# Normalising and turning the second batch's tokens during the first batch's value projection, and choosing PSUM banks by an expected clock

## The chip, the cores and the metric

One core of a Trainium2 chip runs the whole kernel. The metric is the device time of one execution in microseconds (us). Five engines work side by side, each through its own list of instructions in the order in which the program writes them: TensorE (PE) multiplies and transposes into PSUM, VectorE (DVE), ScalarE (ACT) and GpSimd (POOL) work elementwise, and SyncE (SP) only issues DMAs. GpSimd issues DMAs too. An instruction waits until what it reads is written and what it overwrites is read; whatever stands behind it on its engine waits with it.

## The reference: what is computed

`x` has the shape (2, 1024, 1024): two batches of 1024 tokens. All is float32.

```python
xn  = layernorm(x)                                  # no weights
qkv = clip(xn @ Wqkv.T, -8, 8); q, k, v = split(qkv, 3)
q = layer_norm(q, q_ln_w, q_ln_b); k = layer_norm(k, k_ln_w, k_ln_b)
# 32 heads of 32 channels
scores = q @ k.T * 32**-0.5 + slopes * (key - query)    # ALiBi, causal
attn = softmax(scores) @ v
ffn  = xn @ (mean(abs(W), axis=1) * sign(W)).T + bias
out  = x + attn @ Wout.T + ffn
```

## The kernel before, in words

**Projections.** q, k, v and the output projection take seven products instead of eight for each pair of 128-token tiles. The first operand is a pair tile, [128 channels, 7 factors, 4 blocks of channels, 128 tokens]: the tokens, turned so that channels lie on the partitions, as four quarters (A11, A12, A21, A22) and four sums of them (S1 to S4; S3 takes A21's place). `seven` (L413) issues 4 matmuls for each of the seven factors in the order 11, 21, t2, t3, t4, t1, 22 (L210); `combine` (L434) puts the results together on VectorE and ScalarE, with the clip. The weights of a projection, 28 tiles of [128, 512], come through a ring of 28 buffers; `load_weights` (L332) puts the next load on SP's queue when a tile of the projection before has been used for the last time. So k of batch 1 gets its weights while the last pair of v of batch 0 is computed.

**x.** `normalize_x` (L541) takes statistics of a tile on VectorE (L497, L503), the reciprocal root on ScalarE (L507) with a Newton step on VectorE (L513 to L516), and scales on ScalarE (L520). `turn_x` (L546) turns the tile with eight PE transposes (L527, in `transposed`, L524) into two PSUM banks, copied by ScalarE into the pair tile (L554). GpSimd forms the four sums (`add_up`, L399 to L409) and stores the pair tile to DRAM, `xd` (L559, L561, L568), in the layout of the pair tile. q and v, and much later the binarised layer (`prepare`, L755), load it back (`load_pair`, L577). For batch 0 this happens during its k projection, at the start of the kernel. For batch 1 two tiles are loaded and normalised near the end of batch 0's v (in `values`, L663); the rest, all turns, sums and stores lie inside batch 1's k projection.

**k and q.** After the projection, `to_channels` (L584) normalises a row tile, turns it on VectorE in two instructions that transpose every 32x32 block of 128x512 (L592), and stores it with four GpSimd DMAs of 128 KB (L598), whose place in DRAM completes the turn.

**Order of the program.** It is written out by hand. `pieces` (L917) is one long generator: k, q and v of batch 0, the same of batch 1, the binarised layer, the output projection. `fill(time)` (L927) draws from it, counted in the planner's expected times (0.915 us for a projection matmul). The list `sides` holds smaller generators (a tile's normalising, turning, storing); `advance_sides` (L351) moves each by one step for every two pieces. Before the loop over the attention steps the program fills k, q and all but the last 70 matmuls of v of batch 0 (L1270). Then each step issues the loads of keys three steps ahead (`load_keys`, L955), the scaling of keys on ScalarE (`scale_keys`, L964), the first scores (`first_scores`, L1037: four PSUM banks written by PE at L1046, row maxima by VectorE at L1062), the shifts of a block when its maxima are done (`shifts`, L1074: arithmetic on GpSimd, a small PE transpose `trs` at L1088, rows on VectorE), and for the block 9 steps back the second scores (`second_scores`, L1098: PE L1108 and L1122, mask on VectorE L1141, exp on ScalarE L1150), the weighing of values (`weigh_values`, L1181, PE L1190) and the division (`divide`, L1204). Between these, `fill` adds projection matmuls, in a share per step that spreads the projections of batch 1 over the steps (L1256).

**PSUM.** One bank holds the weighed values; the other seven are one rotating pool, and `score_bank` (L372) takes the next in turn for scores, projections (`fill_tile`, L375), transposes (L524) and `trs` (L1088).

Of the kernel before, what the change touches and what calls it, by code (L numbers as in the profile page):

```python
# [19 lines left out]
EPS = 1e-5  # L20
MASKED = -3.0e38
LOWEST = -3.4e38


@with_exitstack
def parallel_block_kernel(
# [33 lines left out]

    nc = tc.nc
    B, S, D = x.shape
    P = 128
    NT = S // P
# [15 lines left out]
    slopes = [2.0 ** (-(h + 1) * ALIBI_BIAS_MAX / N_HEADS) for h in range(N_HEADS)]  # L82

    ctx.enter_context(tc.manual_schedule())
    const = ctx.enter_context(tc.tile_pool(name="const", bufs=1))
    pair_pool = ctx.enter_context(tc.tile_pool(name="pair", bufs=2))
    wpool = ctx.enter_context(tc.tile_pool(name="w", bufs=RING))
    group = ctx.enter_context(tc.tile_pool(name="group", bufs=3))
    work = ctx.enter_context(tc.tile_pool(name="work", bufs=2))
    small = ctx.enter_context(tc.tile_pool(name="small", bufs=4))  # L90
    dram = ctx.enter_context(tc.tile_pool(name="dram", bufs=2, space=bass.MemoryType.DRAM))
    ps_s = ctx.enter_context(tc.tile_pool(name="ps_s", bufs=7, space=bass.MemoryType.PSUM))
    ps_o = ctx.enter_context(tc.tile_pool(name="ps_o", bufs=1, space=bass.MemoryType.PSUM))


    nc.scalar.preload_act_table_set("natural_log_exp_and_others")


    ident = const.tile([P, P], FP, tag="ident", name="ident")
    make_identity(nc, ident)  # L100
    ident_b = const.tile([P, P], BF, tag="ident_b", name="ident_b")
    nc.vector.tensor_copy(ident_b, ident)
    minus_b = const.tile([P, P], BF, tag="minus_b", name="minus_b")
# [111 lines left out]
    def half(n):  # L215
        return slice(n * HALF, (n + 1) * HALF)
# [115 lines left out]
    def load_weights(count):  # L332

        room[0] += count
        while todo and todo[0][0] <= room[0]:
            cost, do = todo.pop(0)
            room[0] -= cost
            do()
# [30 lines left out]
    def half_tile(name):  # L369
        return work.tile([P, HALF], FP, tag="half", name=name, bufs=2)  # L370

    def score_bank(name):  # L372
        return ps_s.tile([P, HALF], FP, tag="s", name=name)

    def fill_tile(name):  # L375
        return score_bank(name)
# [1 line left out]
    def tokens(t):  # L378
        return slice(t * P, (t + 1) * P)

    kd, qd, vd, od, xd = ({} for _ in range(5))
    for b in range(B):
        for what, d in (("k", kd), ("q", qd), ("o", od)):
            d[b] = dram.tile([NC, P, S], FP, tag=f"{what}d", name=f"{what}d_{b}")
        for p in range(NT // 2):
            xd[b, p] = dram.tile([P, 8, NI, P], FP, tag=f"xd{p}", name=f"xd_{b}_{p}")
        vd[b] = dram.tile([S, D], FP, tag="vd", name=f"vd_{b}")

    A11, A12, A22, S3, S1, S2, S4 = range(7)
    A21 = S3
    FACTOR = {"11": A11, "21": A12, "t2": S2, "t3": S3, "t4": A22, "t1": S1, "22": S4}

# [126 lines left out]
            )  # L522

    def transposed(src, c0, what):  # L524
        ps = ps_s.tile([P, 4, P], FP, tag="s", name=f"tr_{what}_{c0}")
        for j in range(4):
            nc.tensor.transpose(  # L527
                ps[:, j, :], src[:, (c0 + j) * P : (c0 + j + 1) * P], ident
            )
        return ps  # L530
# [4 lines left out]
    def load_x(b, t):  # L535
        xin[b, t] = io_tile(f"x_{b}_{t}")
        nc.sync.dma_start(xin[b, t], x[b, tokens(t), :])
# [8 lines left out]
    def turn_x(b, t):  # L546
        p = t // 2
        if t % 2 == 0:
            pairs[b, p] = pair_tile(f"xT_{b}_{p}")
        pr, d = pairs[b, p], xd[b, p]  # L550
        src = xn.pop((b, t))
        for c0, k in ((0, (A11, A21)[t % 2]), (NI, (A12, A22)[t % 2])):
            ps = transposed(src, c0, f"x{b}_{t}")
            nc.scalar.copy(pr[:, k, :, :], ps)  # L554
            yield Turn(TURN) if c0 == 0 else TURN
        if t + 2 < NT:
            load_x(b, t + 2)
        if t % 2 == 0:
            nc.gpsimd.dma_start(d[:, 1:3], pr[:, A11 : A12 + 1])  # L559
        else:  # L560
            nc.gpsimd.dma_start(d[:, 0], pr[:, A21])  # L561
            if (b, p) == (0, 0):
                add_up(pr, nc.vector, 0, NI, lambda: load_weights(NI))
            else:
                add_up(pr, nc.vector if b == 0 and p == 1 else nc.gpsimd, 0, NI)
            done.add(("x", b, p))
            yield 0.0
            nc.gpsimd.dma_start(d[:, 3:], pr[:, A22:])  # L568

    def layernorm(b, t):  # L570
        yield from normalize_x(b, t)
# [9 lines left out]
    W32 = 32  # L581
    BLOCKS = D // W32

    def to_channels(what, b, t, raw, d):  # L584

        name = f"{what}{b}_{t}"
        yield from spread(raw, stats_of(raw, name), name)
        yield 0.0
        dst = work.tile([P, BLOCKS, W32], FP, tag="io", name=f"{what}T_{b}_{t}", bufs=5)
        for n in range(NH2):  # L590
            at = slice(n * BLOCKS // NH2, (n + 1) * BLOCKS // NH2)
            nc.vector.transpose(dst[:, at, :], raw[:, half(n)])  # L592
            yield 0.0
        rows = d[b][:, :, tokens(t)].rearrange("c p s -> (c p) s")
        rows = rows.rearrange("(k r) s -> r k s", r=W32)
        for a in range(P // W32):
            at = slice(a * W32, (a + 1) * W32)
            nc.gpsimd.dma_start(rows[:, :, at], dst[at, :, :])  # L598
        if t == NT - 2:
            done.add((what, b))  # L600

    def projected(what, b, ready):

        if what == "k":
            if b == 0:
                load_x(b, 0)
                load_weights(NI)
                load_x(b, 1)
                load_weights(3 * NI)
                yield from normalize_x(b, 0)  # L610
            yield from turn_x(b, 0)
            if b == 0:
                yield from normalize_x(b, 1)
                load_weights(NI)
        for p in range(NT // 2):
            more = p + 1 < NT // 2
            if what == "k" and more:
                if p > 0:
                    sides.append(layernorm(b, 2 * p + 2))
            elif what != "k" and more:  # L620
                load_pair(b, p + 1)
            elif what in "kq":
                load_pair(b, 0)
            elif b + 1 == B:
                early.extend((signs(), prepare(*every_tile[0])))
                sides.extend(early)
            if (what, b, p) == ("k", 0, 1):
                sides.append(ahead())
            name = f"{what}{b}_{p}"
            rows = [raw_tile(f"{what}raw_{b}_{2 * p + i}") for i in range(2)]  # L630

            def whole(i, src, p=p):
                ready(2 * p + i, src)

            take = combine(name, *rows, whole, bound=CLIP_QKV)
            pr = pairs[b, p]
            args = pr, name, f"{what}{b}", not more, take
            yield from seven(*args, ORDER[:1])
            if what == "k" and p == 0:
                yield from turn_x(b, 1)  # L640
                third = layernorm(b, 2)
                if b == 0:
                    load_weights(1)
                    next(third)
                    load_weights(NI - 1)
                sides.append(third)
            yield from seven(*args, ORDER[1:2])
            if what == "k" and more:
                sides.append(layernorm(b, 2 * p + 3))
            assert ("x", b, p) in done  # L650
            yield from seven(*args, ORDER[2:])
# [11 lines left out]
    def values(b):  # L663
        if b > 0:
            sides.append(residual())

        def ready(t, rows):
            nc.gpsimd.dma_start(vd[b][tokens(t), :], rows)
            if t == NT - 3 and b + 1 < B:
                for i in range(2):  # L670
                    load_x(b + 1, i)
                    sides.append(normalize_x(b + 1, i))
            if t == NT - 2:
                done.add(("v", b))

        return projected("v", b, ready)
# [78 lines left out]
    def prepare(b, t):  # L755

        xt = work.tile([P, NC, P], FP, tag="io", name=f"xt_{b}_{t}", bufs=5)
        d = xd[b, t // 2]
        if t % 2 == 0:
            nc.sync.dma_start(xt.rearrange("p (k c) q -> p k c q", k=2), d[:, 1:3])  # L760
        else:
            nc.sync.dma_start(xt[:, :NI], d[:, 0])
            nc.sync.dma_start(xt[:, NI:], d[:, 3])
        yield 0.0
        hl = []
        for c0 in range(0, NC, NI):
# [307 lines left out]
    def shifts(b, qb, g):  # L1074
# [9 lines left out]
        nc.gpsimd.tensor_tensor(low, sh, mid, ALU.subtract)  # L1084
        yield True

        ps = ps_s.tile([P, P], BF, tag="s", name=f"trs_{b}_{qb}_{g}")
        nc.tensor.transpose(ps, shift_b, ident_b)  # L1088
        rows = small.tile([P, HALF], BF, tag="rows", name=f"rows_{b}_{qb}_{g}", bufs=4)
        nc.vector.tensor_tensor(  # L1090
# [162 lines left out]
    proj = NT // 2 * len(ORDER) * NI * ONE  # L1253


    fills = 3 * proj + AHEAD * ONE + 2 * NT * TURN  # L1256
    share = (fills + sum(time_of(n) for n in range(middle))) / middle
    fills = 1.5 * proj + 2 * ONE + B * NT * 8 * SHORT - BEHIND * ONE
    each = fills / (steps - middle)
# [7 lines left out]
    for n in range(3):  # L1267
        if n in opens:
            load_keys(*opens[n])
    fill(proj - AHEAD * ONE)  # L1270
    chains = []
    for n in range(2):
        if n in opens:
            scale_keys(*opens[n])
    for n in range(steps + 1):
        if n + 3 in opens and not short_lead(opens[n + 3]):
            fill_until(("q", opens[n + 3][0]))
# [88 lines left out]
```

## Time and profile before

| what | us |
|---|---|
| runs, three | 1538.0, 1540.42, 1540.76 |
| their median | 1540.42 |
| the profiled execution's own time | 1538.28 |
| its span, from the first to the last instruction | 1536.5 |
| VectorE turns of keys, 128x512, median | 0.70 |
| landing of the first weights' form, `w_k`, median | 5.6 |
| landing of `xp<-xd`, 1792 KB, median | 8.1 |

The profile is of one execution. A line of it names an engine, the line of the kernel (L527), the operation, and the tiles as output<-input; `idle <- releaser` is how long the engine stood still before it and whose end let it go on. A matmul in float32 leaves two records in the trace. PE's clock was granted at 0.996 on the mean. The DMA lines give, for each kind of transfer, its queue (SPq, POOLq), count, size and the median time to landing:

```profile
xp<-xd SPq DMA_DIRECT2D x16, 1792.0 KB, 8.1
kg<-kd SPq DMA_DIRECT2D x48, 256.0 KB, 4.9
vg<-vd SPq DMA_DIRECT2D x48, 256.0 KB, 5.6
...
xd<-xT POOLq DMA_DIRECT2D x8, 1280.0 KB, 5.2
x<-in_x_dram SPq DMA_DIRECT2D x16, 512.0 KB, 6.1
kd<-kT POOLq DMA_DIRECT2D x64, 128.0 KB, 4.3
```

### The profile page before, as it was taken

How to read it: one execution, taken by the hardware profiler on the slowest of the kernel's cores; microseconds unless marked ns; L12 is line 12 of the kernel's file. 1: busy time of each engine (PE TensorE's matmuls, PEld its weight loads, DVE VectorE, ACT ScalarE, POOL GpSimd, SP SyncE). 2: the span in 40 equal slices, each digit the busy share in tenths (PEclk: the TensorE clock that was granted, in tenths of full speed). 3: DMA queues.
4: the chain of work that ended last, by engine and by line, in shares of the span. 5: the costliest groups of instructions: out<-in, count | busy, mean ns of one | idle time of the engine just before them, and what ended most of it. 6: DMA issues, size and time to landing. Idle time of an engine off the chain costs nothing.

```text
span 1536.5 us, 24276 instructions
## 1 busy us (share of the span) xinstructions
PE 1495.2 (97%) x8100; PEld 636.6 (41%) x8100; DVE 965.9 (63%) x2714; ACT 637.9 (42%) x1219; POOL 1019.2 (66%) x1308
## 2 busy tenths in 40 slices
PE   7999999999999999999999999999999999999998
PEld 3444444444334333333333334555555333333333
DVE  6856553778687766766765565766655565565332
ACT  3322110115556445344444375555555344444430
POOL 4587283025677675796775599877788887777661
PEclk9999999999999999999999999999999999999999
DMA  7788364582333844569842286666668233312232
GB/s 294 273 286 289 95 231 145 194 313 93 114 97 127 260 151 162 102 153 288 260 151 94 106 255 217 144 143 164 144 164 217 72 90 97 88 39 67 59 80 55
DMA packets 118958, 244.88 MB, mean 159 GB/s; under 512 B 12081, under 2 KB 52529, under 8 KB 115505
## 3 DMA queue, kind: packets, MB, share of 16 engines
q1 hardware_dynamic: 90912, 148.94, 28.9%
q0 software_dynamic: 27920, 94.39, 24.9%
q8 instruction: 64, 1.05, 0.3%
q14 instruction: 62, 0.50, 0.1%
HBM read 155.47 MB, written 107.74 MB: 171 GB/s over the span
## 4 chain that ended last, share of the span: by engine, by line
PE 81%; DVE 9%; ACT 4%; issue 3%; POOL 2%; DMA 1%; POOLq 0%; DVEq 0%; ACTq 0%
PE s L1046 9%; PE mm_f L817 8%; PE s L1122 8%; PE mm_q_t L419 8%; PE o L1190 7%; PE mm_o_t L419 7%; PE mm_k_t L419 6%; PE mm_o L419 5%; PE mm_v_t L419 5%; PE mm_v L419 4%; PE mm_q L419 4%; PE mm_k L419 3%; PE s L1108 3%; DVE s L1062 3%; PE den L1209 2%
## 5 line engine op out<-in xcount | busy, mean ns | idle before, releaser
L1179 POOL TENSOR_TENSOR pT<-pT,pT 128x512 f32<-128x512 f32 (+3 forms) x628 | 577.9, 977 | 161.8 <-ACT pT L1150 140.7
L1150 ACT ACTIVATE pT<-s,kpos 128x512 f32<-128x512 f32 (+3 forms) x768 | 378.2, 590 | 440.0 <-DVE s L1141 255.7
L1062 DVE CUSTOM_DVE_ANT_0 s<-s,rel 128x512 f32<-128x512 f32 (+3 forms) x512 | 283.3, 600 | 90.4 <-PE s L1046 84.7
L1046 PE MATMUL s<-kg,qg 32*128 32x512 f32 (+3 forms) x1536 | 174.4, 520 | 0.0
L1062 DVE CUSTOM_DVE_ANT_0 s<-s,rel,mx 128x512 f32<-128x512 f32 (+3 forms) x256 | 140.8, 589 | 42.4 <-PE s L1046 40.1
L1122 PE MATMUL s<-qg,kg 32*128 32x512 f32 (+3 forms) x1536 | 159.6, 495 | 0.0
L1190 PE MATMUL o<-pT,vg 128*32 128x512 f32 (+3 forms) x1536 | 156.3, 494 | 1.3 <-ACT pT L1150 1.3
L817 PE MATMUL mm_f<-sg,hl 128*128 128x512 f32 x512 | 126.7, 399 | 1.7 <-DVE mx L1062 1.7
L1141 DVE TENSOR_TENSOR s<-s,behind 128x256 f32<-128x256 f32 (+1 forms) x320 | 97.9, 374 | 36.9 <-PE s L1122 36.8
L419 PE MATMUL mm_o_t<-w_o_t,ot 128*128 128x512 f32 x256 | 116.5, 602 | 0.0
L1046 PEld LDWEIGHTS s<-kg,qg 32*128 32x128 f32 x1536 | 71.0, 183 | 104.3 <-issue 56.4
L419 PE MATMUL mm_k_t<-w_k_t,xT 128*128 128x512 f32 x224 | 108.9, 614 | 0.0
L419 PE MATMUL mm_v_t<-w_v_t,xp 128*128 128x512 f32 x224 | 106.3, 607 | 2.7 <-POOL w_v_t L236 2.7
L1062 DVE DVE_READ_ACCUMULATOR2_ANT mx<- 128x1 f32 x768 | 108.7, 141 | 0.0
L419 PE MATMUL mm_q_t<-w_q_t,xp 128*128 128x512 f32 x224 | 107.7, 618 | 0.0
L817 PEld LDWEIGHTS mm_f<-sg,hl 128*128 128x128 f32 x512 | 93.4, 188 | 33.6 <-DVE mx L1062 12.0
L1108 PE MATMUL s<-rows,minus_b 12*128 12x512 bf16 (+3 forms) x768 | 77.1, 328 | 17.2 <-DVE mx L1062 16.6
L419 PE MATMUL mm_k<-w_k,xT 128*128 128x512 f32 x192 | 91.5, 615 | 0.3 <-ACT xT L554 0.3
L419 PE MATMUL mm_v<-w_v,xp 128*128 128x512 f32 x192 | 89.9, 604 | 0.0
L419 PE MATMUL mm_q<-w_q,xp 128*128 128x512 f32 x192 | 89.4, 606 | 0.0
L419 PE MATMUL mm_o<-w_o,ot 128*128 128x512 f32 x192 | 87.7, 602 | 0.0
L1190 PEld LDWEIGHTS o<-pT,vg 128*32 128x32 f32 x1536 | 37.3, 108 | 118.8 <-issue 101.7
(169 smaller groups left out, 1756.6 us busy)
## 6 DMA issues: line engine op xcount, KB each, us to landing
xp<-xd SPq DMA_DIRECT2D x16, 1792.0 KB, 8.1
kg<-kd SPq DMA_DIRECT2D x48, 256.0 KB, 4.9
vg<-vd SPq DMA_DIRECT2D x48, 256.0 KB, 5.6
wd_ot<-in_wout_t_dram POOLq DMA_DIRECT2D x11, 1024.0 KB, 9.2
xd<-xT POOLq DMA_DIRECT2D x8, 1280.0 KB, 5.2
x<-in_x_dram SPq DMA_DIRECT2D x16, 512.0 KB, 6.1
kd<-kT POOLq DMA_DIRECT2D x64, 128.0 KB, 4.3
qd<-qT POOLq DMA_DIRECT2D x64, 128.0 KB, 3.3
```

Source lines behind the costliest of these rows:

```text
L419: nc.tensor.matmul(ps, pr[:, FACTOR[block], c, :], W[what, block, c], start=(c == 0), stop=(c == NI - 1),)
L817: nc.tensor.matmul(ps, hl[c // NI][:, m % 2, c % NI, :].bitcast(FR), sg[n, c], start=(m == 0), stop=(m == 2 * NC - 1),)
L1046: nc.tensor.matmul(banks[j][:, c0 : c0 + n], q[r, tokens(i - block[1] * NQ)], k[r, :n], start=True, stop=True,)
L1062: nc.vector.tensor_tensor_reduce(out=banks[j][:, c0 : c0 + n], in0=banks[j][:, c0 : c0 + n], in1=rel[:, o0 : o0 + n], scale=1.0, scalar=m ...
L1108: nc.tensor.matmul(banks[j][:, c0:c1], minus_b[r, :], rows[r, q0:], start=(c0 == 0), stop=False,)
L1122: nc.tensor.matmul(banks[j][:, c0:c1], k[r, tokens(kt % NQ)], q[r, q0:], start=False, stop=(c1 == HALF or (block, kt, q0) == unit[-1]),)
L1141: nc.vector.tensor_tensor(at, at, mask, ALU.add)
L1150: nc.scalar.activation(pT[:, c0:c1], banks[j][:, c0:c1], AF.Exp, bias=kpos[:, h, a : a + 1], scale=slopes[h],)
L1179: eng.tensor_tensor(part_sum, part_sum, pT[j], ALU.add)
L1190: nc.tensor.matmul(po[32 * j : 32 * j + 32, q0:], v[:, kt % NQ, 32 * j : 32 * j + 32], pT[j], start=(kt == 0), stop=(last is not None and ...
L1209: nc.tensor.matmul(ps[32 * j : 32 * j + 32, :], ones, total[j], start=True, stop=True,)
```

## The change

It has two parts.

**Batch 1's tokens.** A side generator, `tokens_ahead`, is started at the beginning of batch 0's v. It loads the eight tiles, normalises them as before, turns each with `turned` (VectorE, two instructions a tile; the function is split out of `to_channels`) and stores it by four DMAs on SP's queue, with runs of 128 bytes in DRAM, into `xc` (blocks, tokens). After every second tile, `sums_ahead` loads the four quarters back by SP (256 KB each), forms the four sums on GpSimd and stores them by GpSimd. The k projection of batch 1 now loads its pairs from there like q and v do, the first one at the end of batch 0's v; the path through `turn_x` is left for batch 0 alone. All loads of batch 1's pairs are in runs of 512 bytes. The factors of a pair tile are put in the order A22, A11, A12, so that each tile's two quarters lie side by side in DRAM.

Counted over the program: PE has 64 transposes less, ScalarE 16 copies less, VectorE 16 turns more. GpSimd has as many sums as before; its x stores go from 24 to 16 for batch 0 and 16 for batch 1. SP has 480 DMAs instead of 436: 32 stores of x, 16 loads of quarters and 4 loads of pairs more, and 8 loads for `prepare` less.

In the new order on SP's queue, the first pair of k1 and the last tiles' stores stand between the loads of k1's first weights, and the loads of the last quarters behind its 24th. On GpSimd's queue, the sums of the second, third and fourth pair stand at the shifts of the first attention blocks (the fourth pair's ahead of the third block's).

**PSUM banks.** While the program is built, thin wrappers around the engines and the pools record every instruction with an expected duration and so an expected clock for each engine (`Clocks`, `Timed`, `Program`, `Ring`; nothing of it runs on the chip). `score_bank` no longer takes the next bank in turn. It takes, of the banks whose last tile has a reader already, the one whose last tile is expected to be idle earliest. `trs` and the transposes draw from it too.

Two lines of the schedule move with it: the planner's share no longer counts the turns, and the first blocks' keys are scaled 28 projection matmuls earlier.

```diff
+class Clocks:
+    def place(self, tile, ring, bufs):
...
+        if len(old) > bufs:
+            self.free[name] = self.ended(old.pop(0))
...
+    def idle_since(self, name):
+        return max((t for both in self.log.get(name, {}).values() for t in both[:2]), default=0.0)
+
+    def unread(self, name):
+        here = self.log.get(name, {}).values()
+        return not here or max(r for w, r, by in here) == 0.0 and all(by == "pe" for w, r, by in here)
...
-    def score_bank(name):
-        return ps_s.tile([P, HALF], FP, tag="s", name=name)
+    NB = 7
+    banks_of = [[] for _ in range(NB)]
+
+    def score_bank(name, shape=(P, HALF), dtype=FP):
+
+        def free_at(n):
+            return clocks.idle_since(banks_of[n][-1]) if banks_of[n] else 0.0
+
+        open_ = [n for n in range(NB) if banks_of[n] and clocks.unread(banks_of[n][-1])]
+        n = min(set(range(NB)) - set(open_), key=lambda n: (free_at(n), used[n]))
+        used[n] = next(count)
+        t = ps_s.tile(list(shape), dtype, tag=f"s{n}", name=name)
+        banks_of[n].append(t[:].tensor.name)
+        return t
...
-            xd[b, p] = dram.tile([P, 8, NI, P], FP, tag=f"xd{p}", name=f"xd_{b}_{p}")
+            if b == 0:
+                xd[b, p] = dram.tile([P, 8, NI, P], FP, tag=f"xd{p}", name=f"xd_{b}_{p}", bufs=1)
+            else:
+                xc[b, p] = dram.tile([8, NC // 2, P, P], FP, tag=f"xc{p}", name=f"xc_{b}_{p}", bufs=1)
+                xd[b, p] = xc[b, p].rearrange("k c p q -> p k c q")
...
-    A11, A12, A22, S3, S1, S2, S4 = range(7)
+    A22, A11, A12, S3, S1, S2, S4 = range(7)
...
+    def turned(name, raw, rows, queue):
+
+        dst = work.tile([P, BLOCKS, W32], FP, tag="io", name=f"{name}T", bufs=5)
         for n in range(NH2):
             at = slice(n * BLOCKS // NH2, (n + 1) * BLOCKS // NH2)
             nc.vector.transpose(dst[:, at, :], raw[:, half(n)])
             yield 0.0
...
-            nc.gpsimd.dma_start(rows[:, :, at], dst[at, :, :])
+            queue.dma_start(rows[:, :, at], dst[at, :, :])
+
+    def tokens_ahead(b):
+
+        for i in range(2):
+            load_x(b, i)
+        for t in range(NT):
+            p = t // 2
+            yield from normalize_x(b, t)
+            yield 0.0
+            k = 2 - 2 * (t % 2)
+            rows = xc[b, p][k : k + 2].rearrange("k c p q -> (k c p) q")
+            yield from turned(f"x{b}_{t}", xn.pop((b, t)), rows, nc.sync)
+            if t + 2 < NT:
+                load_x(b, t + 2)
+            if t % 2 == 1:
+                sides.append(sums_ahead(b, p))
+
+    def sums_ahead(b, p):
+
+        for _ in range(4):
+            yield 0.0
+        d = xd[b, p]
+
+        def part(name, k=None):
+            w = work.tile([P, NI, P], FP, tag="pT", name=f"xs_{b}_{p}_{name}", bufs=16)
+            if k is not None:
+                nc.sync.dma_start(w, d[:, k])
+            return w
+
+        a21, a22, a11, a12 = (part(n, n) for n in range(4))
+        for _ in range(4):
+            yield 0.0
+        s1, s2 = part("s1"), part("s2")
+        nc.gpsimd.tensor_tensor(s1, a21, a22, ALU.subtract)
+        nc.gpsimd.tensor_tensor(s2, s1, a11, ALU.subtract)
+        yield 0.0
+        nc.gpsimd.tensor_tensor(a21, a11, a21, ALU.subtract)
+        nc.gpsimd.tensor_tensor(a12, a12, s2, ALU.add)
+        yield 0.0
+        for k, w in ((S3, a21), (S1, s1), (S2, s2), (S4, a12)):
+            nc.gpsimd.dma_start(d[:, k + 1], w)
+        done.add(("x", b, p))
...
     def projected(what, b, ready):
...
+        if (what, b) == ("v", 0):
+            sides.append(tokens_ahead(b + 1))
         for p in range(NT // 2):
             more = p + 1 < NT // 2
-            if what == "k" and more:
+            if fresh and more:
                 if p > 0:
                     sides.append(layernorm(b, 2 * p + 2))
-            elif what != "k" and more:
+            elif more:
                 load_pair(b, p + 1)
             elif what in "kq":
                 load_pair(b, 0)
-            elif b + 1 == B:
+            elif b + 1 < B:
+                load_pair(b + 1, 0)
+            else:
...
-            if t == NT - 3 and b + 1 < B:
-                for i in range(2):
-                    load_x(b + 1, i)
-                    sides.append(normalize_x(b + 1, i))
...
-        ps = ps_s.tile([P, P], BF, tag="s", name=f"trs_{b}_{qb}_{g}")
+        ps = score_bank(f"trs_{b}_{qb}_{g}", (P, P), BF)
...
-    fills = 3 * proj + AHEAD * ONE + 2 * NT * TURN
+    fills = 3 * proj + AHEAD * ONE
...
-    fill(proj - AHEAD * ONE)
-    chains = []
+    fill(proj - (AHEAD + 28) * ONE)
     for n in range(2):
         if n in opens:
             scale_keys(*opens[n])
+    fill(28 * ONE)
+    chains = []
```

## The prediction

> **What bounds the kernel now.** I read the page's busy line and its shares of the chain first, then the busy time by stage, then the PE timeline where the change removes work, then the waits.
>
> ```profile
> PE 1495.2 (97%) x8100; PEld 636.6 (41%) x8100; DVE 965.9 (63%) x2714; ACT 637.9 (42%) x1219; POOL 1019.2 (66%) x1308
> PE 81%; DVE 9%; ACT 4%; issue 3%; POOL 2%; DMA 1%; POOLq 0%; DVEq 0%; ACTq 0%
> ```
>
> PE is busy 1495.2 of 1536.5 us: 41 us are all that its waits can give back, and beyond that only work taken off PE helps. The chain of waits agrees, with 81% on PE and 9% on DVE.
>
> The stages in question are v of batch 0 (204 to 325 us) and k of batch 1, which runs beside the first attention steps (325 to 490). Columns: stretch, its length, then PE, PEld, DVE, ACT and POOL busy with counts, clock, DMA share, GB/s.
>
> ```profile
> 204.00:265.00 61.00, 58.34 (x135) 25.02 (x133) 25.97 (x46) 7.36 (x12) 36.74 (x45) 1.00 0.59 190
> 265.00:325.00 60.00, 60.00 (x226) 26.09 (x226) 43.46 (x129) 7.47 (x12) 4.86 (x15) 1.00 0.64 218
> 325.00:490.00 165.00, 158.38 (x985) 67.05 (x984) 126.71 (x397) 89.83 (x181) 104.55 (x156) 0.98 0.37 127
> ```
>
> In v0, DVE, ACT and POOL are half idle or more. In k1, DVE is busy 77% of the time and PE stands still for 6.6 us. Batch 1's tokens are normalised and turned almost wholly in k1 today; the change moves that to v0, into the cover, but v0 has the fuller DMA engines (0.59 to 0.64 against 0.37).
>
> **A. Turns leave PE: -7.5 us.** The timeline of PE shows two of the eight turns of k1 (eight transposes each):
>
> ```profile
> 324.49 1.09 PE L527 MATMUL tr_x<-ident,x 128*128 128x128 f32 x8
> 325.87 3.70 PE L419 MATMUL mm_k<-w_k,xT 128*128 128x512 f32 x8 [0.28 <-ACT xT L554]
> 329.41 1.04 PE L527 MATMUL tr_x<-ident,x 128*128 128x128 f32 x8
> 330.28 1.02 PE L419 MATMUL mm_k<-w_k,xT 128*128 128x512 f32 x2
> ```
>
> From start to start the second costs 330.28 - 329.41 = 0.87 us. Eight turns make 8 x 0.87 = 7.0 us. The first also waits for ACT's copy (324.49 to 325.87 = 1.38 us), 0.5 more. All of it lies on PE, which has no other work put in its place: the turn goes to DVE as two transposes of 128x512, the form that the keys use (0.70 us each, 16 in all = 11.2 us), and ACT loses its 16 copies (0.59 each).
>
> The Trainium skill, "VectorE: DVE Perf Modes", section "Rules for kernel authors", speaks against this: a 128x128 transpose belongs on TensorE where a PSUM destination will do. By that rule A would not be there. The rows say 0.87 us of PE a tile against 1.40 us of DVE: VectorE is the slower one here, but it has idle time in v0 and PE has none, so the rows decide.
>
> **B. Less on DVE in k1: -4 us (0 to -11).** The x work takes 2.37 us of DVE a tile, 19.0 us for eight (statistics, Newton steps, part of the spread), plus 23.8 us of ACT. What it does to PE shows at 336 us. DVE:
>
> ```profile
> 336.53 1.27 DVE L497 BATCH_NORM_STATS2 stats_x<-x 128x6 f32<-128x512 f32 x2
> 337.96 1.23 DVE L497 BATCH_NORM_STATS2 stats_x<-x 128x6 f32<-128x512 f32 x2
> ...
> 341.79 0.56 DVE L1062 CUSTOM_DVE_ANT_0 s<-s,rel 128x384 f32<-128x384 f32 x1
> ```
>
> and PE just after:
>
> ```profile
> 342.85 0.37 PE L1108 MATMUL s<-rows,minus_b 12*128 12x512 bf16 x1 [0.55 <-DVE mx L1062]
> 343.76 0.37 PE L1108 MATMUL s<-rows,minus_b 12*128 12x512 bf16 x1 [0.54 <-DVE mx L1062]
> ```
>
> DVE spends some 4.5 us on x before it comes to the maxima that release the score banks, and PE waits for these one by one. Over the kernel I followed each bank in program order: at 100 places PE's next matmul starts within 0.12 us of the end of its bank's last reader, 49.5 us between the starts on the two sides. 17.7 us of it lie between 300 and 510. The five places whose delay holds x work sum to 0.46 + 2.25 + 0.56 + 0.84 + 2.0 = 6.1 us; counting at each place the smaller of the stall and the x work ahead of it gives 11.1. I take 4, two thirds of the five, since attention's own maxima still come late behind the projection's evictions; 0 if those fill the gap.
>
> **C. Banks by expected clocks: -2 us (-4.6 to +3).** Seven shared banks (score_bank) are now picked by an estimate of which was last used earliest. In 45.5 of the 49.5 us no other bank was free either, and taking the bank that was really released first would have saved 4.6 us over the whole kernel. That is the lower end; a wrong estimate can make a wait where there was none, and +3 is the size of the longest single wait on a maximum (2.5 us in the waits view) and a little. The view's total is small too:
>
> ```profile
> PE s L1108 <- DVE mx L1062: 16.6, 31, 2.5
> ```
>
> (us in total, times, longest). The choice hardly moves: bank 1 or 2 by age is picked in 1454 of 1465 cases before and 1400 of 1453 after.
>
> **D. What is added in v0: +2 us (0 to +7 in the forecast; beyond that it is rival 3).**
>
> DVE: 8 x (2.37 + 1.40) - 2 tiles' normalising already there = 25.4 us into 121 - 25.97 - 43.46 = 51.6 idle. POOL: 16 sums at 1.27 and 16 stores at 0.55 = 29.1 into 79.4 idle. ACT moves 23.8 less the copies, into 106 idle. All three fit by sum. PE waits on them only where a piece is late: the sums of the last pair (4 x 1.27 + 4 x 0.55 = 7.3 us) stand on POOL's queue ahead of the third block's shift arithmetic, which feeds PE's trs (L1088). Today a pair's four sums and its stores stand at similar places, so I add 2.
>
> Queues: on SP the stores of x wait for DVE's turns. Behind the last two tiles' stand k1's weights of factors 21, t2 and t3, behind the last pair's part loads the rest of k1's weights and the values of the first block; all of these are issued well ahead of their matmuls, and DVE's turn is late by a few us at most. On POOL the sums wait for the part loads to land (some 5 us, as 256 KB loads of keys do: 4.9 on the page's DMA lines), and behind them stand the shifts of the first blocks.
>
> DMA: the engines are busy 0.66 of 204 to 345, 93 of 141 us. Added, per 16 engines: 32 stores of x by SP with runs of 128 bytes. The same form on POOL's queue exists for the keys:
>
> ```profile
> L598 POOL DMA_DIRECT2D kd<-kT x64: 783/783/834, 53.2 to 574.7; - x64
> L592 DVE STREAM_TRANSPOSE kT<-kraw x32: 656/701/712, 50.7 to 560.9; 128x512 f32<-128x512 f32 x32
> ```
>
> (ns min/median/max; first and last start.) In the packet rows each such store is 32 packets of 4096 bytes at 281 ns, 32 x 281 / 16 = 0.56 us; whole-run packets of that size take 159. So 32 x 0.56 = 18 us. Part loads: 16 x 512 packets of 512 bytes x 27 ns / 16 = 13.8. The first pair of k1: 3584 x 27 / 16 = 6.0. Sum stores: 16 x 128 x 178 / 16 = 22.8. Together 61, so 154 into 141: about 13 us spill beyond 345, where the share is 0.37. The spill delays loads, which wait for nothing if they were early enough: k1's first weights are issued from 297.5 us on and needed at 325.9; the keys of the first steps have 24 us, and today's loads of x among them land in 10.6 us, which leaves 13.
>
> How SP's queue cuts a store with 128-byte runs no row here shows. If it moves each run at the price of a 512-byte packet, a store costs 1024 x 27 / 16 = 1.73 us and all 55; I take 0.56, because it is the same shape, and keep 1.73 for rival 3. The Trainium skill, "DMA: Bandwidth & Descriptors", opening table, puts line rate at 512 bytes and more, and a read-modify-write below; 281 against 159 ns agrees in direction and gives a factor of 1.8, no more. If 128 bytes cost four times the whole-run price (an estimate from that page's figure), the 18 us would be 41.
>
> Cost nothing: sixteen fewer evictions on ACT (not the bound); merged xt loads (8 fewer on SP, in the binary stage, far ahead); keys scaled 28 matmuls earlier (on ACT, busy 7.47 of 60 us there; without that cover, under 2 us); 12 more loads of the later pairs in 512-byte pieces, a pair ahead.
>
> **The sum.** -7.5 - 4 - 2 + 2 = -11.5. The profiled execution took 1538.28 (span 1536.5 and 1.8 around it): 1526.8. It lies 2.1 us under the median of the runs, 1540.42, so on the runs' scale it is 1528.9. I say **1528**, between the two.
>
> **Rivals.**
>
> 1. *The k1 waits dissolve widely.* For it: the 17.7 us of bank waits there, x work ahead of many. Against it: attention's own DVE work stays. -7.5 - 11 - 4.6, with D at nothing, is 1538.3 - 23.1 = **1515**.
>
> 2. *Only the transposes go; a wait takes the place of the one removed* (the change does not do what it says). PE then meets DVE's maxima sooner and stands for them as long, and the estimated banks come out as the old ones. For it: 45.5 of 49.5 us have no free bank. Against it: the stall at 342 us has x work as its cause in plain sight. 1538.3 - 7.5 + 5 (D at its upper part) = **1536**, 1533 to 1541.
>
> 3. *Slower: DMA saturates in 265 to 345 us.* One mechanism: SP's stores with 128-byte runs fill the engines, so that w_k, the first keys and the first pair of k1 land late. With s us for one store, the backlog at 345 is 32 s + 43 + 93 - 141 = 32 s - 5. The cover is 13 us (keys) to 34 (weights, 28 us of lead and what later weights have), and the gain to eat is 13.5 (A, B, C). It turns slower when 32 s - 5 exceeds 26.5 to 47.5, that is from s = 0.98 to 1.64 us. At 1.73 the backlog is 50, the loss 16 to 37 and the time about 1541 to 1562, **1550** in the middle. For it: the share is 0.93 at 325 to 345 already. Against it: the key stores of the same shape cost 0.56.
>
> **Chances.** Forecast (1520 to 1535): 0.53. Rival 1: 0.17. Rival 2: 0.20, of which 0.12 under 1537.3, 0.08 within the bound. Rival 3: 0.10. A measurement of this kernel tells about 0.2%, 3.1 us. Faster: 0.53 + 0.17 + 0.12 = 0.82; same 0.08; slower 0.10. The range 1515 to 1541 takes in the forecast, rival 2 and half of rival 1 and leaves out rival 3: about 0.8.
>
> **What will show it.** A: the turns' rows hold batch 0 alone, 64 transposes, and k1 is 7 us shorter on PE. B: the wait of L1108 on the maxima falls under 10 us, and the one at 342 us is gone. C: bank waits outside k1 change by under 3 us. D: the DMA share in v0 is 0.8 to 0.95, SP's stores land in 5 to 8 us, and no PE wait names a weight or a key in 265 to 345. What would prove me wrong: a wait of mm_k on its weights or of the first scores on kg (rival 3), or DVE stalls of the same sum at other places (rival 2).

## The result, and the profile after

The changed kernel takes 1551.83 us (median of 4, 1549.98 to 1553.6), the kernel before beside it 1540.55: a ratio of 1.0077, 95% interval 1.0059 to 1.0094. It is **slower** by 0.8%, outside the range and on the other side of the forecast. The profiled execution took 1549.98 us (span 1548.2), 11.7 more than that of before.

The page of the changed kernel, the busy line and the chain's shares:

```profile
PE 1492.6 (96%) x8036; PEld 633.5 (41%) x8036; DVE 977.5 (63%) x2730; ACT 631.6 (41%) x1203; POOL 1027.2 (66%) x1316
PE 77%; DVE 9%; DMA 5%; POOL 4%; issue 2%; ACT 2%; SPq 1%; POOLq 0%; DVEq 0%; ACTq 0%
```

PE has its 64 transposes less (8100 to 8036) and still stands idle 55.6 us where it stood 41.3. The chain, which had 1% on DMA, now has 5%, and 4% on POOL. The same stages as before, with the same columns:

```profile
204.00:265.00 61.00, 58.85 (x130) 25.07 (x129) 35.23 (x77) 12.67 (x22) 37.33 (x45) 0.94 0.82 250
265.00:325.00 60.00, 56.89 (x197) 24.59 (x196) 49.69 (x148) 12.24 (x20) 28.21 (x38) 0.97 1.01 287
325.00:490.00 165.00, 150.47 (x903) 60.30 (x905) 115.95 (x348) 66.30 (x136) 82.86 (x132) 0.96 0.54 157
```

The x work has moved: DVE gained 9.3 + 6.2 us in v0 and lost 10.8 in k1. The DMA engines are full from 265 to 325 us (1.01, before 0.64). And the granted clock, 1.00 in v0 before, is 0.94 and 0.97. PE's waits, in total, times, longest (all lines of the changed kernel are L148, where its wrapper issues every instruction; one goes by the tiles):

```profile
PE trs L148 <- POOL shift_b L148: 13.6, 1, 13.6
...
PE s L148 <- DVE mx L148: 6.0, 14, 1.0
PE den L148 <- DVE pT L148: 5.4, 1, 5.4
...
PE mm_v L148 <- DVE mv_x L148: 2.9, 1, 2.9
PE s L148 <- ACT pT L148: 2.9, 1, 2.9
```

The two of these that the kernel before has too:

```profile
PE trs L1088 <- POOL shift_b L1084: 1.9, 1, 1.9
...
PE den L1209 <- DVE pT L1179: 0.6, 1, 0.6
```

The wait that the change was to shorten fell from 16.6 to 6.0 us. Four others came or grew, and one of them alone, 13.6 us, is longer than the whole forecast gain of 11.5.

**The ledger.** For every pair of neighbouring groups of matmuls of the same forms I took the shortest spacing found in the kernels of this study (the 5th percentile) as its price, and the rest as excess. The prices of PE's work fall from 1426.9 to 1420.7 us in the change, and to 1419.3 where PE's order in the second half is that of before. The excess:

| us from the start | before | changed | difference | what it is in the changed kernel |
|---|---|---|---|---|
| 0 to 200 | 7.0 | 7.6 | +0.6 | start, batch 0 |
| 200 to 310 | 4.3 | 12.3 | +8.0 | mm_v waits for DVE; half clock |
| 310 to 360 | 4.7 | 14.9 | +10.2 | trs waits for GpSimd |
| 360 to 700 | 42.3 | 27.8 | -14.5 | the waits on maxima that went |
| 700 to 940 | 13.7 | 15.2 | +1.5 | |
| 940 to 1460 | 23.2 | 27.7 | +4.5 | first scores wait for a bank near 944 |
| 1460 to the end | 1.0 | 8.9 | +7.9 | den waits at the end |
| sum | 96.3 | 114.4 | +18.1 | with -6.2 of prices: +11.9, measured 11.7 |

The prices come from all the kernels compared, so single figures are good to about 1 us. So the gains are there, -6.2 and -14.5, more than forecast, and some 33 us of losses stand against them. Three places show how they arise.

**1. GpSimd's queue, 13.6 us.** The timeline of PE (start, length, instruction, idle time and releaser):

```profile
351.19 1.20 PE L148 MATMUL s<-qg,kg 32*128 32x512 f32 x8
365.99 0.29 PE L148 MATMUL trs<-ident_b,shift_b 128*128 128x128 bf16 x1 [13.59 <-POOL shift_b L148]
```

That of GpSimd in the same stretch:

```profile
333.92 0.54 POOL L148 DMA_DIRECT2D vd<-vraw  x1 [2.29 <-DVE vraw L148]
356.56 1.26 POOL L148 TENSOR_TENSOR xs_s<-xs,xs 128x512 f32<-128x512 f32 x1 [22.09 <-DMA xs<-xc]
...
364.58 0.23 POOL L148 TENSOR_TENSOR sh<-mx,pos 128x16 f32<-128x16 f32 x1
```

And SP's queue ahead of those quarters:

```profile
320.64 7.81 SPq L148 DMA_DIRECT2D xc<-x_6T  x4
...
334.25 8.51 SPq L148 DMA_DIRECT2D xc<-x_7T  x4
342.86 4.61 SPq L148 DMA_DIRECT2D w_k_t<-wd_kt  x9
...
349.87 2.56 SPq L148 DMA_DIRECT2D xs<-xc  x4
```

GpSimd stands 22 us in front of the last pair's first sum, whose quarters SP loads only at 349.9, behind two sets of stores that hold SP for 8 us each and behind weights that wait for their ring. The shift that PE needs stands behind the sums; its last maximum was there at 337.4.

**2. The order of PE in the second half.** At the end PE has nothing between the last exps and den. The change, and then the same den in the kernel before:

```profile
1484.09 3.24 PE L148 MATMUL o<-pT,vg 128*32 128x384 f32 x16 [1.26 <-ACT pT L148]
1492.77 2.49 PE L148 MATMUL den<-pT,ones 128*32 128x512 f32 x8 [5.43 <-DVE pT L148]
```

```profile
1482.07 1.63 PE L1209 MATMUL den<-pT,ones 128*32 128x512 f32 x8 [0.62 <-DVE pT L1179]
```

In the kernel before, 4 projection matmuls stand one step later and den waits 0.62 us. The order of PE's records in the two traces shows that from the second block of batch 1 on the fills run ahead of the attention steps: by 16 records of the binarised layer up to some 1190 us, then by 8 records, which are 4 projection matmuls, until the last step has no fill left. Near 944 ScalarE's casts for the binarised layer, which wait for a load, stand ahead of four exps that hold the banks PE wants:

```profile
945.46 0.62 ACT L148 CAST hl<-xt 128x512 fp32r<-128x512 f32 x1 [3.77 <-DMA vd<-vraw]
945.99 2.42 ACT L148 ACTIVATE pT<-s,kpos 128x512 f32<-128x512 f32 x4
```

(The view names a store of v as the releaser; SP issued the load of xt at 941.64.) In the kernel before, four exps at 939.08 stand ahead of the first cast, at 941.38. I took this stall for a part of the same shift; f1 below shows that it stays when the second half's order is that of before.

**3. The clock.** The stretch that begins within the wait of trs and ends behind it; the clock is the last column but two:

```profile
355.60:369.30 13.70, 3.31 (x5) 1.54 (x6) 0.69 (x1) 1.45 (x3) 10.02 (x18) 0.51 1.08 330
```

And the one behind the wait near 944 us:

```profile
946.50:953.50 7.00, 6.78 (x22) 3.47 (x25) 4.11 (x17) 1.90 (x4) 6.69 (x6) 0.52 0.01 3
```

After a wait of 2.9 us PE works 7 us at half clock, which costs 7.00 x (1 - 0.52) = 3.4 us, more than the wait. Over the kernel the mean clock is 0.986 against 0.996: 2 x 0.014 x 1548 = 43 us at half clock, against 12 before, some of it inside waits, where it costs nothing. (Other executions of the kernel before have mean clocks down to 0.991, so 0.996 is its best.) The Trainium skill, "TensorE: Matmul & The Clock Gate", Part 1, describes a free-running window of 3413 ns and half rate after an idle one; the spells in the change's clock records are one, two or four such lengths (3.4 us at 277, 6.8 at 233 and 946, 13.7 at 356), which agrees. But its advice in "Why this matters for your kernels", no gaps above some 3 us, is too mild for this kernel: 2.9 us were enough, and at 233 us two waits of 0.6 and 1.0 us.

### The profile page after: what moved, and what is told of

Its sections match the earlier page's. It is cut to its first block, busy times and chain, and to the rows that moved or that the text cites. A ratio compares the mean times of both kernels' runs of the same rounds, so it can differ in the third digit from the quotient of the medians.

```text
span 1548.2 us, 24237 instructions
## 1 busy us (share of the span) xinstructions
PE 1492.6 (96%) x8036; PEld 633.5 (41%) x8036; DVE 977.5 (63%) x2730; ACT 631.6 (41%) x1203; POOL 1027.2 (66%) x1316
## 3 DMA queue, kind: packets, MB, share of 16 engines
q8 instruction: 63, 1.03, 0.3%
## 4 chain that ended last, share of the span: by engine, by line
PE 77%; DVE 9%; DMA 5%; POOL 4%; issue 2%; ACT 2%; SPq 1%; POOLq 0%; DVEq 0%; ACTq 0%
PE s L148 19%; PE mm_f L148 7%; PE o L148 7%; PE mm_q_t L148 7%; PE mm_o_t L148 7%; PE mm_k_t L148 6%; PE mm_o L148 5%; PE mm_q L148 4%; PE mm_k L148 4%; PE mm_v_t L148 4%; PE mm_v L148 3%; DVE s L148 3%; PE den L148 2%; DMA x<-in_x_dram 2%; ACT pT L148 1%
## 5 line engine op out<-in xcount | busy, mean ns | idle before, releaser
L148 POOL TENSOR_TENSOR pT<-pT,pT 128x512 f32<-128x512 f32 (+3 forms) x628 | 578.1, 972 | 139.0 <-ACT pT L148 128.1
L148 ACT ACTIVATE pT<-s,kpos 128x512 f32<-128x512 f32 (+3 forms) x768 | 378.2, 589 | 443.7 <-DVE s L148 237.8
L148 DVE CUSTOM_DVE_ANT_0 s<-s,rel 128x512 f32<-128x512 f32 (+3 forms) x512 | 283.1, 599 | 75.6 <-PE s L148 68.8
L148 PE MATMUL s<-kg,qg 32*128 32x512 f32 (+3 forms) x1536 | 179.3, 524 | 3.0 <-ACT pT L148 2.9
L148 DVE CUSTOM_DVE_ANT_0 s<-s,rel,mx 128x512 f32<-128x512 f32 (+3 forms) x256 | 140.9, 589 | 43.1 <-PE s L148 40.8
L148 PE MATMUL o<-pT,vg 128*32 128x512 f32 (+3 forms) x1536 | 157.3, 494 | 2.5 <-ACT pT L148 2.5
L148 PE MATMUL s<-qg,kg 32*128 32x512 f32 (+3 forms) x1536 | 158.2, 494 | 0.0
L148 PE MATMUL mm_f<-sg,hl 128*128 128x512 f32 x512 | 127.2, 399 | 1.7 <-DVE mx L148 1.7
L148 DVE TENSOR_TENSOR s<-s,behind 128x256 f32<-128x256 f32 (+1 forms) x320 | 98.0, 374 | 47.9 <-PE s L148 47.6
L148 PEld LDWEIGHTS s<-kg,qg 32*128 32x128 f32 x1536 | 74.5, 185 | 112.5 <-issue 53.9
L148 PE MATMUL mm_o_t<-w_o_t,ot 128*128 128x512 f32 x256 | 116.5, 601 | 0.0
L148 PE MATMUL mm_v_t<-w_v_t,xp 128*128 128x512 f32 x224 | 109.2, 622 | 2.1 <-POOL w_v_t L148 2.1
L148 DVE DVE_READ_ACCUMULATOR2_ANT mx<- 128x1 f32 x768 | 108.3, 141 | 0.0
L148 PEld LDWEIGHTS mm_f<-sg,hl 128*128 128x128 f32 x512 | 93.5, 188 | 33.8 <-DVE mx L148 11.2
L148 PE MATMUL mm_q_t<-w_q_t,xp 128*128 128x512 f32 x224 | 105.4, 605 | 0.0
L148 PE MATMUL mm_v<-w_v,xp 128*128 128x512 f32 x192 | 91.7, 614 | 3.1 <-DVE mv_x L148 2.9
L148 PE MATMUL mm_q<-w_q,xp 128*128 128x512 f32 x192 | 88.8, 602 | 0.0
L148 PE MATMUL mm_o<-w_o,ot 128*128 128x512 f32 x192 | 88.1, 604 | 0.0
L148 PEld LDWEIGHTS o<-pT,vg 128*32 128x32 f32 x1536 | 37.9, 108 | 122.7 <-issue 103.1
L148 PEld LDWEIGHTS s<-qg,kg 32*128 32x128 f32 x1536 | 74.9, 186 | 19.3 <-issue 8.1
L148 PE MATMUL s<-rows,minus_b 12*128 12x512 bf16 (+3 forms) x768 | 71.1, 328 | 7.5 <-DVE mx L148 6.0
L148 PEld LDWEIGHTS mm_o_t<-w_o_t,ot 128*128 128x128 f32 x256 | 46.7, 190 | 62.9 <-issue 52.4
```

Of the source, the lines that this page charges most:

```text
L148: result = real(*args, **kw)
```

## The experiments

All times are medians; ratios are to the kernel before on the same chip, with 95% intervals. The kernel before had medians of 1538.96 to 1540.55 on the four occasions, so runs of different occasions are compared by their ratios. Three theories: **Q**, the queues (late x holds SP, GpSimd and DVE, and PE behind them); **B**, the bank choice is the loss; **D**, the load on the DMA engines is, wherever things stand. **S**, the shifted fills, was added after the first four.

**e1: the tokens ahead, banks in rotation.**

```diff
-        n = min(set(range(NB)) - set(open_), key=lambda n: (free_at(n), used[n]))
-        t = ps_s.tile(list(shape), dtype, tag=f"s{n}", name=name)
+        return ps_s.tile(list(shape), dtype, tag="s", name=name)   # pool of 7
```

> Batch 1's tokens go ahead as in the change, the PSUM banks stay the old rotating pool of seven. Theory Q (SP's queue is held by transfers in many small packets; the late quarters hold GpSimd's sums, and those the shift that PE's trs waits for): the 13.6 us wait of trs stays at 12 us or more, only the stall of first scores on a bank near 946 us (6.6 us with the half clock behind it) goes, and the bank part's small gains with it: 1544 to 1553. Theory B (the bank choice is the loss): 1536 or less.

1553.04 us, 1.0098 (1.0082 to 1.0115); trs waits 14.0 us. B is out as the cause of this loss. But Q's guess that the stall near 944 us goes with the bank choice is wrong too: it is there, 2.9 us, with rotation.

**e2: the bank choice alone, in the kernel before.**

```diff
-        return ps_s.tile([P, HALF], FP, tag="s", name=name)
+        n = min(set(range(NB)) - set(open_), key=lambda n: (free_at(n), used[n]))
+        t = ps_s.tile(list(shape), dtype, tag=f"s{n}", name=name)   # with Clocks, Timed, Program, Ring
```

> The kernel before with the banks chosen by expected clocks, nothing else. Theory Q: near the kernel before, 1536 to 1546, a gain of at most 4.6 us in k1 against one wrong choice of up to 6.6 us. Theory B: 1548 or more.

1547.96, 1.0053 (1.0041 to 1.0066): by itself it loses 6.3 to 10.2 us. That lies above Q's range and just under B's 1548, and neither had its size. The order of PE is the same, and the wait on maxima is 16.0 us against 16.6: nothing was gained. In the ledger the excess is 3.0 us more in 310 to 360, 4.1 in 500 to 600 and 2.7 in 700 to 800, and the mean clock 0.992 against 0.996, which says little, since the executions of the kernel before beside it have 0.992 to 0.996.

**e3: the last pair's sums later on GpSimd.**

```diff
-        for _ in range(4):
+        for _ in range(4 if p < NT // 2 - 1 else 13):
             yield 0.0
```

> The change with the last pair's sums nine steps of the side list later, so that on GpSimd's queue they stand behind the shifts of the third and the fourth block instead of ahead of both. SP's queue and the DMA load are as in the change. Theory Q, order part: the wait of trs goes, 13.6 us and the half clock behind it, 1535 to 1540. Theory D (the DMA engines, full from 265 to 325 us, are the loss wherever the sums stand): less than 4 us, 1548 to 1553.

1544.1, 1.0030 (1.0019 to 1.0041), 7.2 us less than the change by the ratios, with the DMA engines as full as there (1.03 from 265 to 325 us). The wait of trs is gone, so D is not the loss as a whole; of the 13.6 us, 3.65 come back as a wait of PE for the first block's values, whose load SP issues only at 354.3, behind the quarters and the last weights. Right after it comes a pair in 512-byte pieces: `xp<-xc` is 3584 packets, and the DMA behind it took 6.7 us to issue (the loads around it 0.3 to 0.7).

**e4: x stored by GpSimd.**

```diff
-            yield from turned(f"x{b}_{t}", xn.pop((b, t)), rows, nc.sync)
+            yield from turned(f"x{b}_{t}", xn.pop((b, t)), rows, nc.gpsimd)
```

> The change with the 32 stores of x on GpSimd's queue instead of SP's. The transfers are the same; the keys' stores of this form on that queue are 32 packets of 4096 bytes where SP's were 1024 of 128. Theory Q: SP is free, loads of x and quarters are early, the wait of trs and the waits of DVE on x go: 1528 to 1538. Theory D: the engines save (0.83 - 0.56) x 32 = 9 us of some 150, a gain of 5 us at most: 1546 to 1552. If GpSimd's queue stalls on DVE's turns instead: 1540 to 1550, with the sums as the named wait.

1546.52, 1.0043 (1.0027 to 1.0059). (One of its seven executions took 8313.5 us, for a reason that no record shows; the ratio leaves it out.) The stores matter, 5.2 us by the ratios, but Q's stronger claim failed: trs still waits 11.3 us in all. The last quarters are loaded at 346.9 instead of 349.9, because they stand behind 23 loads of weights that wait for the ring, stores or not. So the wait is the *order* on two queues, SP's and GpSimd's, and not the bulk of the stores.

**f1: the planner's share less one matmul.** The edit brings PE's order in the second half back to that of before.

```diff
-    fills = 3 * proj + AHEAD * ONE
+    fills = 3 * proj + (AHEAD - 1) * ONE
```

> The change with one projection matmul (0.915 us) less in the planner's sum for the first half, so that from the second block of batch 1 on PE's order is again that of the kernel before; in the change the fills run 1 to 4, at one place 16 matmuls ahead there. Theory S (this shift costs two stalls: first scores near 943 us wait for a bank, 2.9 us and the half clock behind it, 6.6 in all; and the last step has no fill, so that den waits 5.4 us for the sum of the exps, 5.4 in all): 1538 to 1542. Rival: the stalls come from the bank choice or from the late x and stay: 1548 or more.

1532.8, 0.9964 (0.9950 to 0.9977): 17.4 us less than the change, by the ratios and between the profiled spans, and **faster than the kernel before**, by one constant. S had 12, and of its two stalls only one went. The same PE instructions, the trs and the last den, start 1.6 us earlier than in the change at 384 us, 7.2 at 582, 8.9 at 898, 8.7 at 970 and 16.1 at the last den, where den now waits 0.6 us; another 1.3 come behind it, since den no longer runs at half clock. So the end gives 8.7. Between 898 and 970, around the stall near 944, nothing is gained: the first scores still wait 4.0 us there for ScalarE's exps (3.3 in f2, 3.0 in f3), and the casts still stand ahead of these. The line in f4, below, which has the same order:

```profile
922.44 3.23 PE L148 MATMUL s<-kg,qg 32*128 32x256 f32 x14 [4.50 <-ACT pT L148]
```

What S did not have are the 5.6 near 500 (three turns of keys no longer stand on DVE ahead of the maxima that PE waits for, a wait of 2.3 us and the clock behind it) and 1.7 between 582 and 898. The 1.6 at the start are what is left of 2.4 near 236, where the same wait on v's weights was this time not followed by half clock, which I don't put down to the edit.

**f2: e3 and f1 together.**

> The last pair's sums later and the share less one matmul, both. If the two losses are separate (sums ahead of the shift 7.7 us as measured, the shift of the fills 12): 1530 to 1535. If they overlap: 1536 or more.

1525.33, 0.9909 (0.9896 to 0.9923). 7.5 us under f1: the losses are separate.

**f3: f2 with rotation.**

> The same as the run with both, with the old rotating pool of banks. If the bank choice loses here what it lost alone (7 us): 1523 to 1528. If it does nothing beside the tokens that go ahead (as the change with rotation suggests, 1.2 us above the change): within 3 us of the run with both.

1522.81, 0.9892 (0.9878 to 0.9905). 2.5 us under f2, intervals overlapping: beside the tokens that go ahead, the bank choice costs little, if anything.

**f5: the tokens half a projection earlier,** with f1's share and rotation; sums where they fall.

```diff
-        if (what, b) == ("v", 0):
-            sides.append(tokens_ahead(b + 1))
...
+            if (what, b, p) == ("q", 0, 2):
+                sides.append(tokens_ahead(b + 1))
```

> Rotation and the share less one matmul, with the tokens started half a projection earlier, at the third pair of batch 0's q; the sums stand where they fall. Theory Q (lateness is the loss, the work itself is covered): the loads, quarters and sums are all early, neither trs nor mm_v waits for them, 1520 to 1527. Theory D (the DMA engines' load is the loss): it moves with them, PE waits elsewhere, 1531 or more.

1523.84, 0.9898 (0.9884 to 0.9911). k1 is clean, no wait of trs or mm_v, but the sums of the quarters now stand among those of v's weights on GpSimd's queue, and PE waits 6.1 and 6.3 us for the latter (14.2 in four waits).

**g1: the kernel before, the share more by one matmul.** The test of S by itself, without x, banks or loads touched.

```diff
-    fills = 3 * proj + AHEAD * ONE + 2 * NT * TURN
+    fills = 3 * proj + (AHEAD + 1) * ONE + 2 * NT * TURN
```

> The kernel before with one projection matmul more in the planner's sum for the first half, nothing else: in k and q of batch 1 the order of PE moves by 2 matmuls at most, from the second block of batch 1 on the fills run 4 to 16 matmuls ahead and the last step has no fill, as in the change. Theory S (the shift of the fills is a loss by itself): a wait of den of 5 us at the end and a stall near 930 us, 1546 to 1552. Rival (the stalls belong to the new path of x or to the banks): 1538 to 1542.

1549.18, 1.0063 (1.0049 to 1.0076): +9.7 us from one constant. Its end is that of the change, line for line of the waits:

```profile
1490.24 2.49 PE L1209 MATMUL den<-pT,ones 128*32 128x512 f32 x8 [5.47 <-DVE pT L1179]
```

That end is the whole loss. At the last den but one g1 is 3.9 us behind the kernel before, and 3.7 of these are the 4 projection matmuls by which it is ahead in its work; at the last den it is 8.2 us behind, and the half clock makes it 10.9 between the profiled spans. A stall of 5.6 us of excess at 924 comes too, but it is another one than that near 944 (the first scores wait for DVE's maxima), and it is made up elsewhere. So S stands for the end of the kernel, and for the stall near 944 it does not.

**f4: f3 with the stores on GpSimd; f6: f5 with all sums five steps later; f7: f6 with the share less two.**

> The run with both repairs and rotation, with the stores of x on GpSimd's queue. If the SP queue's 128-byte packets still cost there (DVE stands for x near 270 us and PE 5.1 us behind it): 1516 to 1520. If the loads of x are late for their place in SP's order, behind loads that wait: within 2 us of that run, 1521 to 1525.

> The earlier start with all sums five steps later behind their loads. In the run without it GpSimd waited for quarters ahead of the sums of v's weights, and PE 12.4 us for those near 222 to 238 us. If that is the order on GpSimd's queue alone: 1510 to 1514. If the DMA load moves the wait elsewhere: 1519 or more.

> The same with the share less two matmuls instead of one, which puts the exps of batch 0's last block ahead of the casts of the binarised layer's second tile on ScalarE's queue, as in the kernel before. If the stall near 922 us (6 us with the half clock) is ScalarE waiting for that tile's load: 4 to 7 us under the run with one matmul. If it is the PSUM banks of the shifted order: no change.

f4: 1516.69, 0.9856 (0.9841 to 0.9872), 5.5 us under f3 by the ratios: with the order repaired the stores on SP cost what they cost in e4, and PE's wait of 5.0 us at 277 is gone. f6: 1516.85, 0.9857 (0.9839 to 0.9875), 6.3 us under f5: of the 14.2 us for v's weights 6.6 stay (2.7 in the kernel before), now because GpSimd waits 6.3 us at 200.5 for the turn of a q tile, which shares DVE with the x work. Order again, on a third queue. f7: 1519.92, 0.9875 (0.9848 to 0.9902), no gain: the stall that it was aimed at, the one near 944 in the change, is gone (PE waits 0.4 us for the exps), but a wait of 5.2 us for DVE near 275 and one for maxima near 911 took its place. Its six times fall into two groups, 1513.8 to 1516.7 and 1523.1 to 1526.4, and the trace is of the longest, so what the edit is worth stays open. f4 and f6 are the fastest, 1.4% under the kernel before. Stages of f4:

```profile
265.00:325.00 60.00, 57.65 (x195) 24.55 (x194) 49.15 (x146) 12.47 (x20) 43.52 (x58) 1.00 0.93 278
325.00:490.00 165.00, 163.40 (x1007) 65.98 (x1006) 128.65 (x393) 77.61 (x156) 89.51 (x141) 1.00 0.58 181
```

PE is busy 163.4 of 165 us in k1 (150.5 in the change, 158.4 before), at full clock.

## Why the prediction was wrong, step by step

Two steps failed most. D priced work on GpSimd's queue by its own length, where PE waited 13.6 us; and the planner's share, a line of the change, had no term at all. A and B, the gains, were there. Of the signs that the prediction named, B's came true (6.0 us, under 10); the wait that did the harm, trs on GpSimd, was on none of its lists.

- **A, -7.5 us: right.** The prices of PE's work fall by 7.6 (1426.9 to 1419.3) where the rest of the order is kept.
- **B, -4 (0 to -11): right in kind, too small.** Between 360 and 700 us the excess falls by 14.5, in f4 by 21.8; the wait of second scores on maxima falls to 6.0 and 3.6 us. I counted only places where x work stood in plain sight before the maximum, and priced a wait without the half clock behind it.
- **C, -2 (-4.6 to +3): wrong.** Alone it costs 6.3 to 10.2. The bound, "the longest single wait on a maximum ... and a little", was no bound. That a few other picks make new waits, each with its clock, fits the places in the ledger but is not shown.
- **D, +2 (0 to +7): wrong by far, and the place had been named.** That the sums of the last pair "stand on POOL's queue ahead of the third block's shift arithmetic" was written down, but priced by their own 7.3 us of work, and down to 2 because today's sums "stand at similar places". What counts is what the first of them *waits* for: 22.1 us, for loads behind 23 weights on SP (the order ahead of the prediction says 24). PE lost 13.6 us in one wait, and 7.2 of the time came back when only the sums were moved (e3). The prediction listed what stands behind the stores on SP, and called it "issued well ahead".
- **The price of a store on SP:** 0.83 us of engines, 1024 packets of 128 bytes at 13 ns by the packet rows, between my 0.56 (GpSimd's queue makes 32 packets of it) and 1.73. By rival 3's own sum the backlog is 32 x 0.83 - 5 = 22 us, short of its 26.5. But the stores also hold SP itself, 4.0 to 8.5 us for a tile's four, which no term had.
- **"Cost nothing" for 12 loads in 512-byte pieces: wrong,** for the same reason: the DMAs behind the first three took 6.8, 6.8 and 4.7 us of SP.
- **Missing altogether: the planner's share.** The change to `fills` is in the diff and in the text on the code, and got no price. It moved PE's order late in the kernel, by the 4 projection matmuls that the end lacks. One constant gets 17.4 us back in the change, 8.7 of them at the end, and the same step in the kernel before loses 9.7 by the ratio, all at the end.
- **Rival 3** has the right sign, with the wrong mechanism: not the engines' backlog, but the order on three queues and the order of PE. That its 1550 lies beside the measured 1551.83 is luck: it needed 1.73 us a store, and at the measured 0.83 its own sum gives no loss.

Left open: what puts the casts ahead of the exps near 944, which f1 did not undo and f7 did; why the bank choice alone costs more than beside the other part (the ledger has only the places), and how much of the v0 loss is engines and how much SP's queue, since f4 relieves both.

## What to carry to other kernels

Price a step that goes onto a queue by what its first instruction waits for, not by its work, and write down who stands behind it on that queue, for each queue that it touches. When a change takes work out of a hand-made schedule, compare the order of the bound engine to the end of the program, since here one constant in the planner's share cost about as much as the edit gained, at the far end of the program. In the traces of this study every wait of PE from 2.9 us on, the one at 8 us aside, was followed by a half-clock spell, and of the shorter ones some were: add 1.7 to 3.4 us to such a wait.

## What the runs showed of the hardware

- The same store to DRAM, 128 partitions' worth in runs of 128 bytes, is 32 packets of 4096 bytes (281 ns in the median) on GpSimd's queue and 1024 packets of 128 bytes (13 ns) on SP's: 0.56 against 0.83 us of the 16 engines.
- SP issues slowly behind many small packets: the third of four such stores took 1.5 to 4.5 us to issue, and the DMAs behind three loads of 3584 packets 6.8, 6.8 and 4.7 us, against 0.3 to 0.4 for most loads of 256 KB.
- A wait of PE of 2.9 us was followed by 6.8 us at half clock, another of 2.9 us by 3.4 us; three short waits on v's weights, 2.6 or 2.7 us in all, were followed by none in some runs (the kernel before, f1).
